# Local attention in a two-layer decoder: one exponential per tile, and products of two head groups in alternation

## The chip, the cores and the metric

The kernel runs on one core of a Trainium2 chip. The metric is the device time of one execution in microseconds (us). The engines are called PE (matrix products), PEld (PE's weight loads), DVE (vector), ACT (scalar), POOL (GpSimd) and SP (which issues DMAs). Each engine works through its own queue in order; a semaphore holds an instruction until what it needs is done.

## What is computed

1024 tokens of width 256 pass through two decoder layers. Only the fourth of the six parts, the local attention of the second layer, changes in its code. It splits each sequence of 256 tokens into 16 blocks of 16, and every block attends to itself, causally, with 8 heads of 64:

```python
qkv = lax.conv_general_dilated(xp, conv_w, window_strides=(1,), padding='VALID', ...) + conv_b
q, k, v = jnp.split(qkv, 3, axis=-1)
...
qh = jnp.einsum('bsd,dhk->bshk', qb, wq) + bq
kh = jnp.einsum('bsd,dhk->bshk', kb, wk) + bk
vh = jnp.einsum('bsd,dhk->bshk', vb, wv) + bv
...
scores = jnp.einsum('bqhk,bshk->bhqs', qh * scale, kh)
scores = jnp.where(causal[None, None], scores, jnp.asarray(-1000000000.0, scores.dtype))
attn = jax.nn.softmax(scores, axis=-1)
ctx = jnp.einsum('bhqs,bshk->bqhk', attn, vh)
mha_out = jnp.einsum('bqhk,hko->bqo', ctx, wo) + bo
...
out = mha_out @ proj_w + proj_b
```

The parts ahead of it are a linear attention, four experts, and a layer that fetches 64 rows of a table per token ("gather" below). The parts behind it are a cross attention with quantised queries, keys and weights over all 1024 tokens (16 heads), and 16 routed experts of which each token takes two.

## The kernel before

The tokens are 8 tiles of 128. The parts are written as Python generators (streams). A small planner, `Clock` (line 52), keeps an estimated time for each engine; `weave` (line 117) always continues the stream that could start first by that estimate, and what it emits goes into the engines' queues in just that order. PE, ACT and DVE keep this order; SP's and GpSimd's issues are placed by the scheduler behind it. `note` (line 81) holds the estimated costs, with `COLUMN` the price of a column of a matrix product, 0.00085 us at first and 0.0015 after `turn`.

The streams that matter here:

- `fetches` (line 689) issues the gather on GpSimd: 64 chunks of eight indirect DMAs, each chunk into one of three buffers `g`. `weigh` (line 700) uses a chunk: DVE multiplies it with `hb` and sums (`z`), ACT takes a tanh (`th`), DVE makes weights `blk`, PE forms eight products into the accumulator `accs`, in strips of 32 rows. Then the buffer is free for the chunk three further on. After 8 chunks a tile of tokens is complete (`added`).
- `locals_` (line 1037) then runs `local_attention` (line 902) on that tile, tile after tile. `queries` (line 997) follows with the queries of the cross attention, and three streams `units` (line 1051) work off its 8 x 16 pairs of tile and head: scores `psc` on PE in a pair of PSUM banks, maximum `mx` on DVE, exponential `e` on ACT, two transposes on PE in a single bank, a cast `qqT` on ACT, eight products into `accs`.
- `cross_out` and `routes` finish the tile; the routed experts (from line 1256) come after all streams.

`Banks` (line 163) hands out the PSUM banks. After `turn` (line 828) there are two pairs and three single banks (`banks(2, 2, 1, 1, 1)`, `bank.single = 4`); local attention and the units' transposes take single ones. A stream that finds none waits.

In `local_attention` the 128 tokens of a tile hold 8 blocks, so scores are taken over all 128 keys and a mask `cmask` (0 or -1e9) leaves the 16 of the own block. Heads lie as four pairs: head 2m+o has rows o*64 to o*64+63 of slice m in `qh` and `kh`. The projection is formed for the queries (part 0), then for the keys (part 1), each in its own bank and each read out by DVE before the next; a value product `pv` follows. Then two inner streams `half(0)` and `half(1)` are forked, one for each o: four score products, mask, maximum, four exponentials of 128 columns with a per-head bias and summed by the accumulator, reciprocal, product with it, four transposes, a copy `prT`, and four products `pc` into rows o*64 on of a bank, copied to `cT`. The output products `pm` and `po` end the tile.

The four exponentials of a half, line 957:

```python
for m in range(4):
    se_.activation(pr[:, m, :], pr[:, m, :], AF.Exp, bias=nm[:, m:m + 1], accum_out=sm[:, m:m + 1])
```

In the profile every instruction that passes through the planner has line 77, so groups are told apart by their tiles. A float32 product appears as two records.

Of the kernel before, what the change touches and what calls it, by code (L numbers as in the profile page):

```python
# [11 lines left out]
F32 = mybir.dt.float32  # L12
# [4 lines left out]
AF = mybir.ActivationFunctionType  # L17
ALU = mybir.AluOpType
AX = mybir.AxisListType
PSUM = bass.MemoryType.PSUM  # L20

P = 128
# [12 lines left out]
AH, AW, ABLK = 8, 64, 16  # L35
# [9 lines left out]
def bc(ap, axis, n):  # L45

    shape = list(ap.shape)
    shape.insert(axis, n)
    return ap.unsqueeze(axis).to_broadcast(shape)


class Clock:
# [14 lines left out]
    class _Engine:  # L67
# [3 lines left out]
        def __getattr__(self, op):  # L71
            emit = getattr(self.engine, op)

            def timed(*args, **kw):
                out = args[0] if args else kw["out"]
                self.clock.note(self.name, op, out, args, kw)
                return emit(*args, **kw)  # L77

            return timed

    def note(self, engine, op, out, args, kw):
        if engine == "sync":
            return
        n, late = math.prod(out.shape[1:]), 0.11
        if engine == "tensor":
            wide = (args[2] if op == "matmul" else args[1]).dtype == F32
            cost, late = max(0.11, n * self.COLUMN) if wide else max(0.03, n * self.COLUMN / 2), 0.17
            if out.shape[0] == 32:
                cost = max(0.06, n * self.COLUMN / 4)
        elif engine == "scalar":  # L90
            scaled, summed = hasattr(kw.get("scale"), "tensor"), "accum_out" in kw
            cost = 0.06 + n * 0.00083 + 0.23 * (scaled or summed) + 0.06 * (scaled and summed)
        elif engine == "gpsimd":
            cost = 1.23
        elif op in ("max", "max_index", "tensor_reduce"):
            src = args[1] if op != "max_index" else args[2]
            cost = (0.15 if op == "max_index" else 0.085) + 0.00104 * math.prod(src.shape[1:])
        elif op == "reciprocal":
            cost = 0.05 + 0.0064 * n
        elif op == "tensor_tensor_scan":  # L100
            cost = 0.1 + 0.0022 * n
        else:
            cost = 0.085 + (0.00054 if op in ("tensor_scalar", "tensor_copy") else 0.00104) * n
        begin = max(self.free[engine], self.t)
        for x in (*args[1:], *kw.values()):
            if hasattr(x, "tensor"):
                at, by = self.made.get(x.tensor.name, (0.0, engine))
                begin = max(begin, at + self.HOP * (by != engine))
        self.free[engine] = begin + cost
        done = begin + cost + late  # L110
        for x in (out, kw.get("accum_out")):
            if x is not None:
                self.made[x.tensor.name] = done, engine
        self.end = max(self.end, done)
        self.last = engine
# [89 lines left out]
def decoder(ctx, tc, a, out):  # L205


    nc = tc.nc
    ck = Clock(nc)
# [14 lines left out]
    def load(pool, name, shape, view=None, dtype=F32):  # L224
        s = pool.tile(shape, dtype, name="w_" + name, tag="w_" + name)
        nc.sync.dma_start(s, a[name] if view is None else view)
        return s
# [600 lines left out]
    def turn():  # L828

        yield "vector", lambda: None if 0 in fronts_left or 2 in fronts_left or not kv_done else max(kv_done[0], known[5])  # L830
        bank.closing = True
        yield "vector", lambda: None if bank.held else 0.0
        banks(2, 2, 1, 1, 1)
        even_ctx.close()
        wb = ctx.enter_context(tc.tile_pool(name="wb", bufs=1))
        A.conv_w = load(wb, "conv_w", [P, 2, 3 * 192], rows("conv_w"))
        A.conv_bqk = load(wb, "conv_bqk", [P, 1])
        A.conv_bv = load(wb, "conv_bv", [AW, 1])
        A.wqk = load(wb, "wqk", [P, AH * AW])
        A.bq = load(wb, "bq", [P, 4])  # L840
        A.bk = load(wb, "bk", [P, 4])
        A.wv = load(wb, "wv", [AW + 1, AH * AW])
        A.wo = load(wb, "wo", [P, 4, AW], rows("wo"))
        A.bo = load(wb, "bo", [AW, 1])
        A.proj_w = load(wb, "proj_w", [AW + 1, D])
        A.wq = load(wb, "wq", [P, 2, D], rows("wq"))
        A.bq_b = load(wb, "bxq", [P, D], a["bxq"].to_broadcast([P, D]))
        A.work = ctx.enter_context(tc.tile_pool(name="work", bufs=1))
        A.q3 = A.work.tile([P, XH, 4, XD], BF16, name="q3", tag="q3")
        nc.vector.memset(A.q3, 0.0)  # L850

        A.vT = A.work.tile([AW + 1, P], F32, name="vT", tag="vT")
        nc.vector.memset(A.vT[AW:AW + 1, :], 1.0)
        A.mT = A.work.tile([AW + 1, P], F32, name="mT", tag="mT")
        nc.vector.memset(A.mT[AW:AW + 1, :], 1.0)

        A.xp = [A.work.tile([P, 2, P + 2], F32, name=f"xp{i}", tag=f"xp{i}") for i in range(2)]
        nc.vector.memset(A.xp[0][:, :, 0:2], 0.0)
        A.turned = ck.end
        bank.single = 4  # L860
        ck.COLUMN = 0.0015
        yield "vector", None
# [39 lines left out]
    def local_attention(t):  # L902
# [15 lines left out]
        se_.activation(vT[0:AW, :], pqk[0:AW, 1, :], AF.Identity, bias=A.conv_bv)  # L918
        bank.give(pqk)
        yield "tensor", None  # L920
        qh = work.tile([P, 4, P], F32, name="qh", tag="qh")
        kh = work.tile([P, 4, P], F32, name="kh", tag="kh")
        for part, lo in ((0, 0), (1, AW)):
            p = yield from bank.take([P, 4, P])
            for m in range(4):
                te_.matmul(p[:, m, :], A.wqk[lo:lo + AW, m * P:(m + 1) * P], qk[lo:lo + AW, :], start=True, stop=True)
            yield "vector", None
            if part == 0:

                for m in range(4):  # L930
                    ve_.tensor_scalar(qh[:, m, :], p[:, m, :], A.bq[:, m:m + 1], 0.125, ALU.add, ALU.mult)
            else:
                ve_.tensor_tensor(kh, p, bc(A.bk, 2, P), ALU.add)
            bank.give(p)
            yield "tensor", None
        pv = yield from bank.take([P, AH * AW])
        te_.matmul(pv, vT, A.wv, start=True, stop=True)
        yield "scalar", None
        vh = work.tile([P, AH * AW], F32, name="vh", tag="vh")
        se_.copy(vh, pv)  # L940
        bank.give(pv)
        cT = work.tile([P, 4, P], F32, name="cT", tag="cT")

        def half(o):

            psc = yield from bank.take([P, 4, P])
            for m in range(4):
                te_.matmul(psc[:, m, :], qh[o * AW:(o + 1) * AW, m, :], kh[o * AW:(o + 1) * AW, m, :], start=True, stop=True)
            yield "vector", None
            pr = work.tile([P, 4, P], F32, name="pr", tag="pr", bufs=2)  # L950
            ve_.tensor_tensor(pr, psc, bc(cmask.rearrange("p g j -> p (g j)"), 1, 4), ALU.add)
            bank.give(psc)
            nm = work.tile([P, 4], F32, name="nm", tag="nm", bufs=2)
            ve_.tensor_reduce(nm, pr, AX.X, ALU.max, negate=True)
            yield "scalar", None
            sm = work.tile([P, 4], F32, name="sm", tag="sm", bufs=2)
            for m in range(4):
                se_.activation(pr[:, m, :], pr[:, m, :], AF.Exp, bias=nm[:, m:m + 1], accum_out=sm[:, m:m + 1])
            yield "vector", None
            ve_.reciprocal(sm, sm)  # L960
            ve_.tensor_tensor(pr, pr, bc(sm, 2, P), ALU.mult)
            yield "tensor", None
            tp = yield from bank.take([P, 4, P])
            for m in range(4):
                te_.transpose(tp[:, m, :], pr[:, m, :], ident)
            yield "scalar", None
            prT = work.tile([P, 4, P], F32, name="prT", tag="prT", bufs=2)
            se_.copy(prT, tp)
            bank.give(tp)
            yield "tensor", None  # L970
            pc = yield from bank.take([P, 4, P])
            for m in range(4):
                h = 2 * m + o
                te_.matmul(pc[o * AW:(o + 1) * AW, m, :], vh[:, h * AW:(h + 1) * AW], prT[:, m, :], start=True, stop=True)
            yield "scalar", None
            se_.copy(cT[o * AW:(o + 1) * AW], pc[o * AW:(o + 1) * AW])
            bank.give(pc)

        yield "tensor", None
        yield from ck.fork(half(0), half(1))  # L980
        yield "tensor", None
        pm = yield from bank.take([AW, P])
        for m in range(4):
# [456 lines left out]
```

## Time and profile before

| what | us |
|---|---|
| median of 3 runs | 1138.81 (1138.35 to 1142.45) |
| profiled execution | 1261.94 |
| its span | 1260.2 |
| first gather issue on GpSimd | 112.0 |
| start of local attention's first step for tile 0 (`xp` copied) | 421.7 |
| last gather issue | 971.0 |
| last products of the gather, `accs<-g,blk` | 997.5 |
| start of the last tile's output product (`w_proj_w`) | 1049.4 |
| first product of the routed experts' map (`pmap`) | 1143.1 |

The profiled execution took 123 us more than the median. The mean granted clock of PE was 0.708 of full speed.

The profile's page gives busy time and instruction count of each engine, and groups of instructions with their busy time, the mean duration of one in ns, and the engine's idle time ahead of them with what ended it. The busy time of a group is the union of its records: where records run side by side, it is less than their number times their mean. Further views list waits (who waited for whom: us in total, times, longest), busy times by stretch, and the instructions in order of time.

### The profile page before, as it was taken

To read this page: it belongs to the slowest core of one execution; us is meant where nothing else is said; L and a number is where in the kernel's file an instruction comes from. 1 tells how busy PE (TensorE), PEld (TensorE's weight loads), DVE (VectorE), ACT (ScalarE), POOL (GpSimd) and SP (SyncE) were. 2 spreads that over 40 slices of the span, in tenths; PEclk is the share of its full clock that TensorE was granted. 3 is DMA by queue.
4 is the path that set the end of the run, shared out by engine and by line. 5 is a ranking of instruction groups with operands and counts; after the bars stand their busy time and mean duration, and the time that the engine had idled before them with its cause. 6 is when DMAs were issued, how large, how long until landed. Compare 5 with 4: busy or idle time off the path is not lost. (4 is left out here: it accounts for less than half of the span.)

```text
span 1260.2 us, 15565 instructions
## 1 busy us (share of the span) xinstructions
PE 846.4 (67%) x4945; PEld 520.3 (41%) x4945; DVE 821.5 (65%) x2437; ACT 514.4 (41%) x1039; POOL 571.3 (45%) x589
## 2 busy tenths in 40 slices
PE   4672488627834686765688677676786699856990
PEld 3561365414622464333345334343353365323550
DVE  5568667596578458896677775767776767633222
ACT  1241033302301143453575643757456586731220
POOL 2003656575566556576465664655665000002314
PEclk8885588857965877565667866667777566556995
DMA  5012456666556446668665564555665230001323
GB/s 200 1 39 58 135 140 168 188 169 165 138 162 173 134 134 168 172 175 251 167 173 160 162 182 134 149 147 145 179 168 159 87 136 1 5 4 47 84 65 107
DMA packets 68640, 164.67 MB, mean 131 GB/s; under 512 B 15131, under 2 KB 32780, under 8 KB 68557
## 3 DMA queue, kind: packets, MB, share of 16 engines
q0 software_dynamic: 34688, 105.94, 29.9%
q1 hardware_dynamic: 33868, 57.72, 16.6%
q8 instruction: 40, 0.66, 0.2%
q14 instruction: 44, 0.35, 0.1%
HBM read 156.93 MB, written 6.68 MB: 130 GB/s over the span
## 5 line engine op out<-in xcount | busy, mean ns | idle before, releaser
L77 POOL DMA_INDIRECT g<-in_table,idxT x512 | 524.7, 1025 | 438.2 <-issue 153.4
L77 DVE TENSOR_REDUCE mx<-bank 128x1 f32<-128x1024 f32 x128 | 155.8, 1217 | 65.9 <-PE bank L77 51.7
L77 ACT ACTIVATE e<-bank,nb,qs_q 128x1024 uint8<-128x1024 f32 x128 | 154.3, 1206 | 56.1 <-DVE nb L77 22.0
L77 PE MATMUL accs<-g,blk 128*32 128x256 f32 x1024 | 103.9, 542 | 96.5 <-DVE blk L77 69.8
L77 ACT CAST qqT<-bank 128x1024 bf16<-128x1024 uint8 x128 | 127.6, 1010 | 87.9 <-PE bank L77 52.1
L77 PE MATMUL bank<-kT,qT 64*128 64x512 bf16 x256 | 104.2, 518 | 20.8 <-ACT e L77 15.4
L1312 POOL DMA_INDIRECT xr<-xs,smap x24 | 22.7, 948 | 189.5 <-DVE smap L1299 148.4
L77 PEld LDWEIGHTS accs<-g,blk 128*32 128x32 f32 x1024 | 34.5, 141 | 147.3 <-DVE blk L77 77.1
L77 PE MATMUL bank<-ident,e 128*128 128x128 f32 x256 | 72.6, 387 | 32.1 <-ACT e L77 19.0
L77 PE MATMUL accs<-vi,qqT 128*128 128x16 bf16 x1024 | 47.5, 174 | 56.6 <-ACT qqT L77 34.9
L77 DVE TENSOR_TENSOR g<-g,hb 128x1024 f32<-128x1024 f32 x64 | 78.3, 1223 | 8.7 <-issue 5.5
L77 PEld LDWEIGHTS <-qqT 128*128 128x128 bf16 x1024 | 39.8, 103 | 103.7 <-ACT qqT L77 58.9
L77 DVE TENSOR_REDUCE z<-g 128x8 f32<-128x1024 f32 x64 | 78.1, 1220 | 2.2
L77 PEld LDWEIGHTS bank<-ident,e 128*128 128x128 f32 x256 | 36.0, 185 | 85.6 <-issue 35.1
L77 ACT ACTIVATE th<-u 128x16 f32<-128x16 f32 x64 | 13.9, 218 | 90.8 <-DVE u L77 82.0
L77 PE MATMUL bank<-ident,ln_xn 128*128 128x128 f32 x96 | 25.0, 378 | 33.3 <-ACT ln_xn L77 17.1
L77 ACT ACTIVATE ln_xn<-x,ln_nmr,ln_rstd 128x256 f32<-128x256 f32 x48 | 27.0, 595 | 37.4 <-DVE ln_nmr L77 33.1
L77 PE MATMUL bank<-xnT,w_w_up 128*128 128x256 f32 x128 | 35.8, 441 | 7.6 <-ACT xnT L77 4.3
L1321 PE MATMUL ph<-w,xrT 128*128 x96 | 38.9, 513 | 1.8 <-DVE xrT L1318 1.7
L77 PE MATMUL bank<-w_ctxT,aT 128*128 128x256 f32 x128 | 34.3, 421 | 6.7 <-issue 5.1
L77 DVE TENSOR_SCALAR nb<-mx,nsq,ln 128x1 f32<-128x1 f32 x128 | 34.9, 273 | 4.6
L1325 DVE TENSOR_TENSOR hd<-hd,ph 128x176 f32<-128x176 f32 x24 | 8.0, 337 | 42.9 <-ACT hd L1324 42.9
(293 smaller groups left out, 1686.3 us busy)
## 6 DMA issues: line engine op xcount, KB each, us to landing
hb<-hdram SPq DMA_DIRECT2D x128, 256.0 KB
g<-in_table,idxT POOLq DMA_INDIRECT x512
w<-in_w SPq DMA_DIRECT2D x16, 352.0 KB
ys<-yr SPq DMA_DIRECT2D x24, 128.0 KB
w_w2a<-in_w SPq DMA_DIRECT2D x1, 2048.0 KB
x<-in_x SPq DMA_DIRECT2D x8, 128.0 KB
w_ctxT<-in_ctxT SPq DMA_DIRECT2D x1, 1024.0 KB
w_w_up<-in_w_up SPq DMA_DIRECT2D x1, 1024.0 KB
```

The costliest lines, as they stand in the source:

```text
L77: return emit(*args, **kw)
L1312: nc.gpsimd.indirect_dma_start(out=xr, out_offset=None, in_=xs, in_offset=bass.IndirectOffsetOnAxis(ap=smap[:, i:i + 1], axis=0))
L1321: nc.tensor.matmul(ph.rearrange("p j n -> p (j n)"), xrT[:, k, :], w13[:, bass.ds(e, 1), k, :], start=(k == 0), stop=(k == 1))
L1325: nc.vector.tensor_tensor(hd, hd, ph[:, 1, :], ALU.mult)
```

## The change

The local attention of a tile is rewritten as one stream without the fork.

- The products of o = 0 (rows 0 to 63) and o = 1 (rows 64 to 127) are issued in alternation, in two banks, for the projections (queries and keys) and for the scores; the products of the values alternate between output rows 0 to 63 and 64 to 127 of one bank.
- The query bias is added in one DVE operation of 512 columns, with a bias scaled beforehand (`bq8`).
- After the mask, DVE takes the maximum over the 8 key blocks of a row, which leaves the 16 columns of the own block for each of 8 heads (`sc`, 128 columns), then the maximum over these, and subtracts it. ACT takes one exponential of the 128 columns. DVE sums, inverts, multiplies, and spreads the result back to 8 x 128 columns by a product with a 0/1 mask `seen`.
- The value product `pv` stands behind the scores. `cT` is copied at once.
- `note` counts a product that is marked `halves` at 0.55 of its cost; `COLUMN`, `HOP`, `LANDS` and the other constants stay.

```diff
+                kw.pop("halves", None)
                 return emit(*args, **kw)
...
+            elif kw.pop("halves", False):
+                cost *= 0.55
...
+        A.bq8 = wb.tile([P, 4], F32, name="bq8", tag="bq8")
+        nc.vector.tensor_scalar(A.bq8, A.bq, 0.125, None, ALU.mult)
...
+        A.seen = A.work.tile([P, P // ABLK, ABLK], F32, name="seen", tag="seen")
+        nc.vector.tensor_scalar(A.seen, cmask, -0.5, None, ALU.is_ge)
...
+        p = []
+        for part in range(2):
+            p.append((yield from bank.take([P, 4, P])))
+        for m in range(4):
+            for part in range(2):
+                lo = part * AW
+                te_.matmul(p[part][:, m, :], A.wqk[lo:lo + AW, m * P:(m + 1) * P], qk[lo:lo + AW, :],
+                           start=True, stop=True, halves=True)
+        yield "vector", None
+
         qh = work.tile([P, 4, P], F32, name="qh", tag="qh")
+        ve_.scalar_tensor_tensor(qh, p[0], 0.125, bc(A.bq8, 2, P), ALU.mult, ALU.add)
+        bank.give(p[0])
         kh = work.tile([P, 4, P], F32, name="kh", tag="kh")
...
+        ve_.tensor_tensor(kh, p[1], bc(A.bk, 2, P), ALU.add)
+        bank.give(p[1])
+        yield "tensor", None
+
+        psc = []
+        for o in range(2):
+            psc.append((yield from bank.take([P, 4, P])))
+        for m in range(4):
+            for o in range(2):
+                te_.matmul(psc[o][:, m, :], qh[o * AW:(o + 1) * AW, m, :], kh[o * AW:(o + 1) * AW, m, :],
+                           start=True, stop=True, halves=True)
+        yield "vector", None
+        pr = work.tile([P, AH, P // ABLK, ABLK], F32, name="pr", tag="pr")
+        for o in range(2):
+            ve_.tensor_tensor(pr[:, 4 * o:4 * o + 4].rearrange("p m g j -> p m (g j)"), psc[o],
+                              bc(cmask.rearrange("p g j -> p (g j)"), 1, 4), ALU.add)
+            bank.give(psc[o])
+
+        sc = work.tile([P, AH, ABLK], F32, name="sc", tag="sc")
+        ve_.tensor_reduce(sc, pr.rearrange("p h g j -> p h j g"), AX.X, ALU.max)
+        sm = work.tile([P, AH], F32, name="sm", tag="sm")
+        ve_.tensor_reduce(sm, sc, AX.X, ALU.max)
+        ve_.tensor_tensor(sc, sc, bc(sm, 2, ABLK), ALU.subtract)
+        yield "tensor", None
         pv = yield from bank.take([P, AH * AW])
         te_.matmul(pv, vT, A.wv, start=True, stop=True)
         yield "scalar", None
+        se_.activation(sc, sc, AF.Exp)
...
+        ve_.tensor_reduce(sm, sc, AX.X, ALU.add)
+        ve_.reciprocal(sm, sm)
+        ve_.tensor_tensor(sc, sc, bc(sm, 2, ABLK), ALU.mult)
+        ve_.tensor_tensor(pr, bc(sc, 2, P // ABLK), bc(A.seen, 1, AH), ALU.mult)
...
+        pc = yield from bank.take([P, 4, P])
+        for m in range(4):
+            for o in range(2):
                 h = 2 * m + o
...
+                te_.matmul(pc[o * AW:(o + 1) * AW, m, :], vh[:, h * AW:(h + 1) * AW], prT[o][:, m, :],
+                           start=True, stop=True, halves=True)
+        yield "scalar", None
+        cT = work.tile([P, 4, P], F32, name="cT", tag="cT")
+        se_.copy(cT, pc)
```

More of the change, by code (lines that the diff above doesn't have):

```diff
@@ L922, in local_attention @@
+        bank.give(p[0])
         kh = work.tile([P, 4, P], F32, name="kh", tag="kh")
[L923 to L935, printed above, removed]
+        ve_.tensor_tensor(kh, p[1], bc(A.bk, 2, P), ALU.add)
@@ L941, in local_attention @@
         bank.give(pv)
[L942 to L962, printed above, removed]
+        yield "vector", None
@@ L963, in half @@
+        ve_.tensor_reduce(sm, sc, AX.X, ALU.add)
+        ve_.reciprocal(sm, sm)
+        ve_.tensor_tensor(sc, sc, bc(sm, 2, ABLK), ALU.mult)
+        ve_.tensor_tensor(pr, bc(sc, 2, P // ABLK), bc(A.seen, 1, AH), ALU.mult)
+        yield "tensor", None
+        prf = pr.rearrange("p h g j -> p h (g j)")
+        prT = []
+        for o in range(2):
             tp = yield from bank.take([P, 4, P])
             for m in range(4):
-                te_.transpose(tp[:, m, :], pr[:, m, :], ident)
+                te_.transpose(tp[:, m, :], prf[:, 4 * o + m, :], ident)
@@ L966, in half @@
             yield "scalar", None
-            prT = work.tile([P, 4, P], F32, name="prT", tag="prT", bufs=2)
-            se_.copy(prT, tp)
+            prT.append(work.tile([P, 4, P], F32, name="prT", tag=("qh", "kh")[o]))
+            se_.copy(prT[o], tp)
             bank.give(tp)
             yield "tensor", None
-            pc = yield from bank.take([P, 4, P])
-            for m in range(4):
+        pc = yield from bank.take([P, 4, P])
+        for m in range(4):
+            for o in range(2):
@@ L973, in half @@
                 h = 2 * m + o
[L974 to L980, printed above, removed]
+                te_.matmul(pc[o * AW:(o + 1) * AW, m, :], vh[:, h * AW:(h + 1) * AW], prT[o][:, m, :],
+                           start=True, stop=True, halves=True)
@@ L981, in local_attention @@
+        yield "scalar", None
+        cT = work.tile([P, 4, P], F32, name="cT", tag="cT")
+        se_.copy(cT, pc)
+        bank.give(pc)
         yield "tensor", None
```

## The prediction

> **What bounds the kernel now.** I read the busy shares first, then what GpSimd waits for, then busy times by stretch, then the local attention's own instructions, then one stall in order of time, and last the chain of waits of the end.
>
> ```profile
> PE 846.4 (67%) x4945; PEld 520.3 (41%) x4945; DVE 821.5 (65%) x2437; ACT 514.4 (41%) x1039; POOL 571.3 (45%) x589
> ...
> L77 PE MATMUL accs<-g,blk 128*32 128x256 f32 x1024 | 103.9, 542 | 96.5 <-DVE blk L77 69.8
> ...
> L77 PE MATMUL bank<-xnT,w_w_up 128*128 128x256 f32 x128 | 35.8, 441 | 7.6 <-ACT xnT L77 4.3
> ```
>
> No engine is full over the span, so the limit must be looked for by stage. From 112 to 972 us GpSimd issues 512 indirect gathers in 64 chunks of eight. Each chunk takes three buffers in turn, so chunk n starts only when the products `accs<-g,blk` of chunk n-3 are done.
>
> ```profile
> POOL g L77 <- PE accs L77: 113.7, 28, 9.6
> ```
>
> In order of time on GpSimd, a chunk's eight gathers take 10.3 us in the mean, and the pause ahead of a chunk that isn't late is about 1.3 us: 11.6 us is GpSimd's own pace. I summed what the pauses have above 1.3 us: 79 us from 412 us on, and 68 of these lie inside the seven stretches in which a local attention (tiles 0 to 6) is under way. The busy times by stretch show the same: GpSimd has 31.50 of 58 us (54%) while tile 5's local attention runs, and 19.22 of 27 us (71%) between two of them.
>
> ```profile
> 826.00:884.00 58.00, 44.58 (x343) 26.80 (x344) 40.48 (x85) 36.42 (x72) 31.50 (x32) 0.75 0.53 146
> 924.00:967.00 43.00, 35.16 (x259) 22.96 (x258) 32.32 (x56) 28.69 (x59) 28.45 (x28) 0.80 0.57 162
> ...
> 562.00:589.00 27.00, 12.69 (x98) 5.35 (x98) 20.79 (x65) 13.05 (x25) 19.22 (x19) 0.54 0.79 233
> ```
>
> (Columns: stretch, its length, busy us of PE, weight loads, DVE, ACT, POOL, then granted clock, DMA share, GB/s.) One stall, of tile 3:
>
> ```profile
> 690.42 2.72 PE L77 MATMUL bank<-kh,qh 64*128 64x128 f32 x15
> ...
> 693.07 1.50 PE L77 MATMUL accs<-g,blk 128*32 128x256 f32 x16
> ...
> 694.96 0.95 POOL L77 DMA_INDIRECT g<-in_table,idxT  x1 [8.49 <-PE bank L77]
> ```
>
> The chunk's weights `blk` were ready at 690.0, but its products stood in PE's queue behind 3.0 us of score products (690.04 to 693.07), and GpSimd got its buffer only after them. Earlier the same chunk had lost time in ACT's queue (its tanh waited from 683.3 to 688.6 behind a cast that waited for PE).
>
> The second place is the tail. Tile 7's last chunk is added at 998.25; its local attention runs to about 1050, its queries to 1069, then 16 units of its cross attention to 1117, then routing and the expert stage (1138 to 1260), which the change doesn't touch. Everything up to about 421 us is the same order as before.
>
> **The change part by part, per tile.**
>
> ```profile
> L77 ACT ACTIVATE pr<-pr,nm 128x128 f32<-128x128 f32 x64 | 24.8, 393 | 3.1 <-DVE nm L77 3.1
> L77 PE MATMUL bank<-kh,qh 64*128 64x128 f32 x128 | 24.7, 429 | 0.0
> ...
> L77 PE MATMUL bank<-qk,w_wqk 64*128 64x128 f32 x128 | 22.3, 321 | 11.0 <-ACT qk L77 9.3 <-DVE qh L77 1.1 <-issue 0.5
> L77 PE MATMUL bank<-prT,vh 128*64 128x128 f32 x128 | 20.5, 326 | 0.2 <-ACT xnT L77 0.2
> ```
>
> ACT: eight exponentials go, 24.8 / 8 = 3.1 us a tile (each one's accumulator read overlaps the next). One of 128 columns without accumulator comes: between the row of 64 columns (0.26) and the 0.39 of 128 columns with accumulator, I take 0.32. Two copies into `cT` of 0.58 become one of 128x512, 0.58 by the row of `vh`. ACT loses 2.8 + 0.6 = 3.4 us.
>
> PE: 67.5 us in the three rows above, 8.4 a tile, is to run two products at a time. The trace has such a pair: while tile 3's halves meet (691.07 to 691.9) records of the two halves start between each other, and each half keeps its own step of 0.213 us. Four strips of 32 columns are the other row: 103.9 / 1024 = 0.101 us a record against 35.8 / 128 = 0.280 for full 256-column records, 2.8 times for four strips, 69% of ideal. For two I take 1.7 times: 8.4 becomes 4.9, 3.5 us less. Bounds: 0 (no overlap) to 4.2 (twice).
>
> Here a rule speaks against the gain. "TensorE: Matmul & The Clock Gate" (Part 1, on the clock gate) says that the array's clock is halved unless recent activity holds it up. The rows agree in direction: PE busy 47% goes with a clock of 0.54 (562:589), 82% with 0.80 (924:967), a slope of 0.26 / 0.35. Taking 3.5 us out of about 57 us of stretch is 6 points of busy time, by that slope 0.045 of clock, so the other 33 us of PE in the stretch would take 2 us longer: 1.5 us gained instead of 3.5. But a low clock also lengthens what is counted as busy, and the gaps in these stretches come from waits that the change shortens; I keep 3.5 and let the range carry 1.5.
>
> DVE: out go four `qh` (9.0 / 8 = 1.1), two maxima of 0.69, two reciprocals (0.34), two products of 0.69; in come one `qh` of 512 (0.69 by `aT`), a maximum over 1024 (1.22 by `z<-g`), four operations of at most 128 columns (0.28 or so each), a reciprocal (0.20) and a product of 1024 (1.22). 6.3 becomes 6.5 us: no gain on the engine that is busiest by count, 425 of 598 us between 400 and 998. The maximum reads one float in 16. "SBUF — State Buffer" (the note on cachelines in the port section) says that reads which leave a 16-byte line each time pay; no row here has such a read by DVE. By the row it is 1.22; if the read costs double, 2.44, which is 10 us of DVE over eight tiles. I take 1.22, the row of the same count, and keep both.
>
> What moves: the value product stands behind the scores now; PE's scores wait for both `qh` and `kh`; the exponential waits for the maxima of all eight heads. Behind the scores on PE stand the next chunk's `accs` and the units, so a late `kh` holds both; before, a late `qh` held them at the second projection in the same way. The two added setup operations of DVE (a scaled bias, a 0/1 mask) run once: 0.3 us. They stand at about 405 us, while the bias's load is issued at 238.5, so there is no wait. SP and GpSimd issue the same transfers; only some of SP's `hb`, `hdram` and `xs` change places.
>
> **The sum**, against the profiled execution (1261.9 us, span 1260.2):
>
> - Gather stage. A local attention has about 17.7 us of PE work, 8.1 of ACT and 10.4 of DVE with its normalisation, 36 in all; the change takes out 3.5 + 3.4 - 0.2 = 6.7, or 19%. In the stall shown, 3.0 us of scores would become 1.7, 1.3 of 7.2 us lost, again 18%. So I take 20% of the 68 us: 14 us. Bounds: 0, and all 6.7 us on seven tiles, 47.
> - Tail. Tile 7's exponentials are on the chain of the end for 2.6 us, of which 2.3 go; PE's three groups give 3.8 (2.2 + 2.6 + 3.9 become about 5), one copy 0.6. Against it the chain loses the overlap of its halves: mask and maxima take 3.2 us instead of 1.3 before the exponential can start, normalising 2.0 instead of 0.9. Net 6.7 - 3.0, about 4 us.
>
> 18 us of 1262, 1.4%. The runs without a profile have a median of 1138.8, 0.902 of the profiled one, and no view tells where the difference lies; with the same factor the gain is 16 us and the time **1122 us**. Its own range, from half to twice the gain: 1106 to 1131.
>
> **Rivals.**
>
> *Slower: banks.* Units and local attention share three single PSUM banks. Before, a projection held one; now two are held from the first projection to the mask (672.7 to 695.3 for tile 3), and the units' transposes, which keep a bank some 2 us through the cast, have one left. Against it: the scores of the two halves already held two, and the planner places takes when it thinks them free. PE's queue stands with a transpose that waits. With five units in that stretch and eight tiles, each us that they wait is 40 us: from 0.45 us on the 18 us are eaten, and at 1 us the sum is 22 us over: 1159 us.
>
> *No change: DVE.* If without a profile GpSimd is quicker than here, DVE at over 70% paces the stage and neither ACT nor PE matters; only the tail's 4 us stay: 1135, and with the doubled maximum 1144.
>
> *More: all stalls of the removed work go.* 47 + 7 = 54 us, 1090. For it: the waits sit exactly in those stretches. Against it: much of them is PE at half clock in the convolution and `w_wp` products, which stay.
>
> *The pairs don't overlap.* Then PE gives nothing, ACT alone half of it: 8 us, 1132.
>
> **How the numbers follow.** A measurement tells 0.5% (5.7 us) from no change. Forecast 0.51, more 0.09, no overlap 0.08: faster 0.68. DVE's case 0.12 for the same, 0.04 for slower with the doubled maximum; banks or an unlucky new order of the queues 0.16. The range 1096 to 1154 leaves out most of the "more" case and the bad half of the banks' case.
>
> **What would show it.** Right: records of `bank<-kh,qh` and `bank<-qk,w_wqk` starting in pairs, and the three groups busy for some 40 us (67.5 / 1.7); ACT's busy time down by about 27 us; GpSimd's pauses above 1.3 us after 412 us near 65 us instead of 79; `sc<-pr` at 1.22 us. Wrong: the wait of `g` for `accs` not smaller, transposes `bank<-ident,e` idle after a bank's release, the mean clock well below 0.708, or the last `accs<-g,blk` not earlier than 998.

## The result and the profile after

| what | before | changed |
|---|---|---|
| median, first chip | 1138.58 (1136.96 to 1142.45, 4 runs) | 1155.07 (1154.42 to 1159.61, 4 runs) |
| profiled execution | 1261.94 | 1159.61 |
| its span | 1260.2 | 1157.9 |
| first gather of chunk 22 | 395.3 | 358.8 |
| last products of the gather end | 998.1 | 894.9 |
| from there to the end of the span | 262.1 | 263.0 |

The changed kernel takes 1.015 of the time before, 95% interval 1.0119 to 1.0182: 16.5 us more, where 16 less were forecast. (A ratio here and below is taken over the undisturbed runs of both kernels, so it can differ a little from the ratio of the medians beside it.) The profiled executions can't be set against each other. The one of before took 123 us more than the median of its kernel and is none of its timed runs; on which chip it was taken is not on record. The one of the changed kernel took 4.5 us more than its median. By chunk 22 they are already 36.5 us apart, and up to there both kernels issue the same work in the same order.

The profile's page of the changed kernel, engines first, then the gather's products:

```profile
PE 812.9 (70%) x4945; PEld 494.7 (43%) x4945; DVE 826.2 (71%) x2423; ACT 490.7 (42%) x911; POOL 567.6 (49%) x589
...
L78 PE MATMUL accs<-g,blk 128*32 128x256 f32 x1024 | 100.5, 529 | 80.1 <-DVE blk L78 75.1
```

PE is busy 33.5 us less and ACT 23.7 less; DVE has 4.7 more. The mean granted clock is 0.713, before 0.708. These differences too are between executions of different length; pairs from one chip follow in the part on the prediction. The groups that the prediction sized, from the groups of the changed kernel:

```profile
L78 DVE TENSOR_REDUCE sc<-pr 128x128 f32<-128x1024 f32 x8 | 15.0, 1872 | 0.3
...
L78 PE MATMUL bank<-prT,vh 128*64 128x128 f32 x128 | 14.7, 400 | 0.0
...
L78 PE MATMUL bank<-kh,qh 64*128 64x128 f32 x128 | 13.0, 340 | 1.3 <-DVE kh L78 1.3
...
L78 PE MATMUL bank<-qk,w_wqk 64*128 64x128 f32 x128 | 11.7, 287 | 0.9 <-ACT qqT L78 0.6
...
L78 DVE TENSOR_TENSOR pr<-sc,seen 128x1024 f32<-128x1024 f32 x8 | 9.8, 1225 | 0.3
...
L78 ACT ACTIVATE sc<-sc 128x128 f32<-128x128 f32 x8 | 2.5, 316 | 11.2 <-DVE sc L78 11.2
```

The three product groups are busy for 39.4 us instead of 67.5, and the exponential takes 0.316 us. The maximum that reads one float in 16 takes 1.872 us, while the spread of the same 1024 columns takes 1.225. The last row also shows a new wait: ACT idles 1.4 us a tile until DVE has the maximum of all eight heads.

GpSimd's wait for the buffers, and the busy times of the gather stage from chunk 23 on and of the rest:

```profile
POOL g L78 <- PE accs L78: 65.5, 28, 7.1
```

```profile
382.00:895.00 513.00, 391.82 (x2842) 222.70 (x2834) 419.06 (x1053) 284.29 (x487) 335.53 (x332) 0.69 0.67 180
895.00:1157.00 262.00, 185.29 (x877) 101.03 (x877) 120.09 (x356) 106.82 (x210) 38.21 (x41) 0.66 0.21 64
```

(Same columns as in the prediction.) In this stage DVE is busy 419 of 513 us (82%), PE 76%, GpSimd 65%. The wait of `g` is 65.5 us against 113.7. Most of that belongs to the condition of the execution, which the next part is about: on the two chips where both kernels have a profile, this wait falls by 15.6 us (130.8 to 115.2, chip B) and 15.9 us (144.3 to 128.4, chip D).

### The profile page after: what moved, and what is told of

Read it like the earlier page. It is cut to its first block, busy times and chain, and to the rows that moved or that the text cites. A ratio compares the mean times of both kernels' runs of the same rounds, so it can differ in the third digit from the quotient of the medians.

```text
span 1157.9 us, 15402 instructions
## 1 busy us (share of the span) xinstructions
PE 812.9 (70%) x4945; PEld 494.7 (43%) x4945; DVE 826.2 (71%) x2423; ACT 490.7 (42%) x911; POOL 567.6 (49%) x589
## 5 line engine op out<-in xcount | busy, mean ns | idle before, releaser
L78 PE MATMUL accs<-g,blk 128*32 128x256 f32 x1024 | 100.5, 529 | 80.1 <-DVE blk L78 75.1
L78 PE MATMUL bank<-kT,qT 64*128 64x512 bf16 x256 | 106.7, 522 | 33.5 <-ACT e L78 29.0
L78 PE MATMUL bank<-ident,e 128*128 128x128 f32 x256 | 73.9, 388 | 23.2 <-ACT e L78 15.2
L78 DVE TENSOR_TENSOR g<-g,hb 128x1024 f32<-128x1024 f32 x64 | 78.3, 1224 | 10.3 <-DMA g<-in_table,idxT 5.7
L78 PE MATMUL accs<-vi,qqT 128*128 128x16 bf16 x1024 | 47.2, 175 | 27.1 <-ACT qqT L78 24.6
L78 PEld LDWEIGHTS <-qT 64*128 64x128 bf16 x256 | 17.3, 101 | 54.6 <-issue 46.9
L1347 DVE TENSOR_TENSOR hd<-hd,ph 128x176 f32<-128x176 f32 x24 | 8.0, 336 | 42.8 <-ACT hd L1346 42.8
L78 PEld LDWEIGHTS bank<-ident,ln_xn 128*128 128x128 f32 x96 | 13.6, 182 | 55.1 <-ACT ln_xn L78 38.6
```

The lines of the kernel that those rows point to most:

```text
L1347: nc.vector.tensor_tensor(hd, hd, ph[:, 1, :], ALU.mult)
```

## Two conditions of the same kernel

On every other chip that was used, the kernel before took 1268 to 1295 us (medians; on the last chip two runs at 1271 and 1277), close to its first profiled execution and not to its 1138. It is not the profiler that makes it slow there: the medians of A to D are over 23 to 55 runs, and a profiled one among them does not stand out (on B 1284.54 beside 1292.93). Their profiles have waits that the views put down to "remote": no instruction of the program ends them. The list of waits of the kernel before, on the second of these chips (us in total, times, longest):

```profile
ACT qqT L77 <- remote: 39.5, 9, 8.4
...
ACT kT L77 <- remote: 21.8, 2, 13.5
...
ACT qk L77 <- remote: 14.0, 1, 14.0
```

All such waits in the list come to 175 us there, and to 139 in the profile that the prediction was read from (sums over the engines, over 200 rows; the rest adds up to 4 us). In the profile of the changed kernel on the first chip there is none. In the other 19 profiles each is a wait of ACT, DVE or GpSimd, none begins before the first gather is issued, and none ends more than 2.2 us after the last one. In the profile that the prediction was read from, 57 us of them lie ahead of chunk 22. One of them in order of time, in the changed kernel as it is, on the second chip:

```profile
132.68 0.79 PE L78 MATMUL bank<-headones,rk 128*128 128x8 f32 x3
...
142.49 0.95 POOL L78 DMA_INDIRECT g<-in_table,idxT  x1 [0.30 <-issue]
146.30 0.19 DVE L78 TENSOR_SCALAR rden<-bank 128x32 f32<-128x32 f32 x1 [10.99 <-remote]
146.39 1.01 ACT L78 COPY kT<-bank 128x1024 bf16<-128x1024 bf16 x1 [11.09 <-remote]
```

and the same `rden` in the profile on the first chip:

```profile
135.44 0.18 DVE L78 TENSOR_SCALAR rden<-bank 128x32 f32<-128x32 f32 x1
```

`rden` needs the products `bank<-headones,rk`, which are done by 133.7 in both. On the first chip DVE goes on at 135.44; on the second it stands for 10.99 us, ACT beside it for 11.09, and both go on 2.9 us after the last of eight gathers has been issued (142.49 + 0.95). That the news of PE's work comes late while GpSimd issues is what this looks like ("late signals" in the recorded expectations); the trace doesn't show the cause.

Three marks, from GpSimd's instructions in order of time, one execution each ("pauses" is what GpSimd's pauses ahead of chunks 23 to 64 have above 1.3 us, "remote" all waits of that kind):

| execution | chunk 22 | pauses | last products | from there to the end | remote |
|---|---|---|---|---|---|
| before, first profile | 395.3 | 79.5 | 998.1 | 262.1 | 139 |
| changed, first chip | 358.8 | 33.6 | 894.9 | 263.0 | 0 |
| before, chip B | 401.5 | 102.1 | 1022.4 | 260.3 | 175 |
| changed, chip B | 404.9 | 83.2 | 1014.1 | 263.3 | 173 |
| before, chip D | 401.7 | 106.4 | 1024.6 | 259.6 | 179 |
| changed, chip D | 403.1 | 90.8 | 1017.6 | 260.3 | 155 |

Over six profiles of the kernel before the pauses run from 79.5 to 106.4 us; a seventh, of an execution of 1300.78 us, has 113.8. That is wider than the 14 us which the prediction wanted to see move.

## The experiments

Five more chips, A to E; "before" is the kernel before on the same chip. Theories: *pairs and banks* (the alternating products hold two single banks, the units wait), *DVE* (it paces the stage, and the change adds to it), *order* (the planner's estimate places the queues badly), and *chip* (the forecast was read from waits that the first chip doesn't have). The recorded expectations also name *chain* (the one stream has a longer chain of dependent steps than two halves side by side) and *landing* (the gathers' data land late). The kernel before against itself tells how far a ratio can be trusted: 0.9949 (0.9909 to 0.9989) on A, 1.0016 (0.9984 to 1.0048) on B and 1.0045 (1.0004 to 1.0087) on C. Ratios of different chips that lie less than a per cent apart are not told apart.

### Chip A: one part undone

The kernel before itself.

> The kernel before, unchanged, for a second profile: in the first one the gathers of the second chunk landed 10 us later than in the changed kernel's profile, before the two orders part. If that was that one execution (A), this profile has a span near 1137 us and the last products of the gather at about 875 us, and its pauses of GpSimd above 1.3 us are far below 79 us after the turn. If the profile itself slows this kernel (B), the span is again near 1260.

1293.35 us beside 1288.81. Its profile is the one with 113.8 us of pauses and has 204 us of remote waits.

The changed kernel with full cost in the planner:

```diff
-                cost *= 0.55
+                cost *= 1.0
```

> The changed kernel with the same instructions; only the planner counts the paired products at their full cost again (factor 1.0 for 0.55). If the new order is what costs (order), the time moves by 5 us or more, either way. If the single softmax chain costs (chain) or the two held banks do (banks), it stays within 5 us of 1155.

1274.56 us, 0.9925 (0.9898 to 0.9952).

The changed kernel without alternation in its three places, both banks still held:

```diff
-        for m in range(4):
-            for part in range(2):
+        for part in range(2):
+            for m in range(4):
...
-                           start=True, stop=True, halves=True)
+                           start=True, stop=True)
```

> The changed kernel with the products of o = 0 ahead of those of o = 1, at full cost: no pairs, two banks held as before. If pairs help as forecast (3.5 us of PE a tile), this is 5 to 15 us slower than the changed kernel, 1160 to 1170. Chain: about the same as the changed kernel, 1155. Order: anything within 15 us of it, with no relation to the PE time that is lost.

1277.16 us, 0.995 (0.9921 to 0.998).

The kernel before with alternating projections and scores, the eight exponentials and the two inner streams kept:

```diff
+        p = []
+        for part in range(2):
+            p.append((yield from bank.take([P, 4, P])))
+        for m in range(4):
+            for part in range(2):
+                lo = part * AW
+                te_.matmul(p[part][:, m, :], A.wqk[lo:lo + AW, m * P:(m + 1) * P], qk[lo:lo + AW, :],
+                           start=True, stop=True, halves=True)
...
+        pscs = []
+        for o in range(2):
+            pscs.append((yield from bank.take([P, 4, P])))
```

> The kernel before with pairs in projection and scores, two banks held for both, and the forked halves with their eight exponentials left as they were. Chain: 1130 to 1138, as the loss lies in the new softmax. Banks: 1150 or more, as the two banks are held here too. Order: anywhere from 1125 to 1160.

1305.12 us, 1.0134 (1.0052 to 1.0216). The pairs alone bring no gain. The two versions with one exponential lie where the kernel before lies against itself here (0.9949): no loss is to be seen, against the measured 1.015 of the first chip. The changed kernel itself did not run on this chip, so what its pairs are worth can't be read here.

### Chip B: the changed kernel again, and the estimate

> The kernel before, unchanged, to have its profile from the same chip as the three that follow. If gathers land fast here, a chunk's products on DVE start 10 to 12 us after its last issue, the time is near 1138 and the last products of the gather end near 875 us. If they land slowly, 18 to 22 us, near 1289 and 1030.

1293.29 us beside 1292.93.

The changed kernel as it is:

> The changed kernel, unchanged, beside the kernel before. Theory 'landing': the change's sign depends on how the gathers land; where they land slowly its stalls are those of the first profile, and it is 0.5 to 1.5% faster than before (ratio 0.985 to 0.995); where they land fast, 1.012 to 1.018. Theory 'chain': slower by 1% or more on both.

1285.65 us, 0.9986 (0.994 to 1.0031): the loss of the first chip is not there. That is neither the gain that *landing* wanted (0.985 to 0.995) nor the loss of 1% or more that *chain* wanted on every chip.

The kernel before, and after it the changed kernel, with a higher price of a column:

```diff
-        ck.COLUMN = 0.0015
+        ck.COLUMN = 0.0017
```

> The kernel before, but the planner counts a column of a product at 0.0017 us in place of 0.0015 after the turn: same instructions, other order. Theory 'order': moves by 0.5% or more, either way, as much as the change itself. Theories 'chain' and 'banks' : within 0.5% of before.

1289.89 us, 1.0007 (0.9968 to 1.0045).

> The changed kernel with a column at 0.0017 us. Theory 'order': moves by 0.5% or more against the changed kernel, either way, and may end below the kernel before. Theory 'chain' and 'banks': stays within 0.5% of the changed kernel.

1279.91 us, 0.9932 (0.9882 to 0.9982). The estimate moves the kernel before by nothing, where *order* expected 0.5% or more, and the changed one by half a per cent, with intervals that meet. On this chip there is no loss to be undone, so whether the order costs 1.5% on the first chip stays open.

### Chip C: the same three versions once more

> The kernel before on a third chip. Where PE's signals come without the long delays of the first profile (no stretch over 1.5 us with PE, DVE and ACT all idle between 110 and 1040 us, as in the changed kernel's profile), its time is near 1138 and its profile shows where it is ahead of the changed kernel: 'chain' expects that GpSimd pauses less while a local attention runs; 'order' that the gain lies in a few single stalls of weigh. Where the delays are there, near 1290.

1271.28 us beside 1267.72.

> The changed kernel without pairs (o = 0 ahead of o = 1, full cost). Where before is near 1138: 'chain' 1150 to 1160, like the changed kernel; 'pairs cost' 1138 or less; 'order' anything from 1130 to 1170. Where before is near 1290: ratio about 0.995, as on the first chip.

1275.2 us, 1.0179 (1.0076 to 1.0282).

> The kernel before with pairs in projection and scores only, eight exponentials kept. Where before is near 1138: 'chain' 1130 to 1140; 'banks' 1150 or more; 'order' anything from 1130 to 1170. Where before is near 1290: ratio about 1.013, as on the first chip.

1281.59 us, 1.0211 (1.0105 to 1.0317).

> The changed kernel with the planner's factor for pairs at 1.0: the same instructions in another order. Where before is near 1138: 'order' moves by 5 us or more from 1155; 'chain' and 'banks' stay within 5 us. Where before is near 1290: ratio about 0.99, as on the first chip.

1270.11 us, 1.0116 (1.0002 to 1.0231). The kernels with one exponential take what they took on A, within 0.4% (1275.2 and 1277.16; 1270.11 and 1274.56). The kernel before is 1.6% quicker here (1267.72 and 1288.81), and with it the sign of the ratio turns. The pairs alone are slower on both chips. The kernel before itself is not steady here: in a later session one run took 1286.95 us.

The kernel before once more on this chip:

> The kernel before, for its profile on a chip where signals between engines aren't late. There the time is near 1138, no wait is ended from outside the program's instructions ('remote' 0 us, as in the changed kernel's first profile, where the first profile of before has 139), and the last products of the gather end near 875 us: then the two profiles can be laid side by side. Otherwise near 1270 to 1290 with 130 us or more of such waits.

1273.13 us, with 91.0 us of pauses and 141 us of remote waits; the other profile of it on this chip has 101.0 and 187.

### Chip D: the two halves of the change

The changed kernel with the projections of queries and keys in one bank each, one read out and given back before the other is taken, as before:

```diff
-        for m in range(4):
-            for part in range(2):
-                lo = part * AW
-                te_.matmul(p[part][:, m, :], A.wqk[lo:lo + AW, m * P:(m + 1) * P], qk[lo:lo + AW, :],
-                           start=True, stop=True, halves=True)
+        for part, lo in ((0, 0), (1, AW)):
+            p = yield from bank.take([P, 4, P])
+            for m in range(4):
+                te_.matmul(p[:, m, :], A.wqk[lo:lo + AW, m * P:(m + 1) * P], qk[lo:lo + AW, :], start=True, stop=True)
...
+            bank.give(p)
```

> The changed kernel with the projection as before: the queries into one bank, read out and given back, then the keys into one bank. The scores and the values keep their alternating products, the softmax keeps its one exponential. Theory 'banks' (two single banks held from the projection on make the units' transposes wait): this is faster than the changed kernel on the same chip by 1% or more, 0.98 to 0.99 of it. Theory 'orders' (the planner places each version by an estimate that is off, and any edit draws a new order): it differs from the changed kernel by up to 1% either way, with no relation to the banks. Theory 'DVE' (DVE paces the gather stage and its work is the same here): within 0.5% of the changed kernel.

1319.45 us, 1.0215 (1.0135 to 1.0294).

The same, with scores in one bank at a time too and no alternation anywhere: one exponential alone.

> The changed kernel's softmax (one exponential of 128 columns, the spread by the mask) without any alternating products: projections, scores and values of o = 0 and then of o = 1, one single bank at a time in projection and scores. It is the other half of the version with the pairs alone, which was slower than before by 1.3% and 2.1%. Theory 'pairs' (the alternating products, with the two banks that they hold, cost what was lost): this is not slower than before, 0.985 to 1.00, and faster than the changed kernel on the same chip by 0.5% or more. Theory 'DVE' (the one exponential brings 0.65 us of DVE work a tile more than was counted, on the engine that is fullest): within 0.5% of the changed kernel or slower than it. Theory 'orders': anywhere within 1% of the changed kernel.

1306.24 us, 1.0085 (1.0048 to 1.0123).

> The changed kernel itself, so that the two versions beside it are compared with it on the same chip. It was 1.015 of before where that took 1138 us and 0.9986 where it took 1293. If the ratio goes with the condition of the chip: above 1.01 where before takes less than 1150 us, near 1.00 where it takes more than 1280.

1288.33 us, 0.9913 (0.9878 to 0.9948).

> The kernel before with a profile. Where it takes about 1138 us, the theory of late signals says: hardly any wait that nothing in the program ends (139 us in the first profile of before, 0 in that of the changed kernel), GpSimd's pauses above 1.3 us near 50 us over all chunks and not 123, the last products of the gather near 875 us. Where it takes 1260 us or more: 130 to 190 us of such waits, as in the other profiles.

1285.94 us, 179 us of remote waits. The waits of the version with one bank and then of one exponential alone; the changed kernel had 128.4 us in this row on the same chip:

```profile
POOL g L78 <- PE accs L78: 155.9, 29, 12.9
```

```profile
POOL g L78 <- PE accs L78: 161.3, 29, 13.3
```

The theory of banks wanted the first to be faster than the changed kernel. It is 3% slower. The second, which takes out all pairs, is 1.7% slower. Both are more than the 1% that *order* allowed. On this chip, where the complete change is even a little faster than before, each edit that takes a part out makes it worse, so neither part is found to cost anything here. Yet these two have also the most remote waits, 225 and 273 us against 155, so their ratios may say as much of this condition as of their work. Whether one bank costs time on the first chip was not measured.

### Chip E: a last profile of the kernel before

> The kernel before once more with a profile. Where it takes about 1138 us, the theory of late signals says: hardly any wait that nothing in the program ends, GpSimd's pauses above 1.3 us near 50 us over all chunks, the last products of the gather near 875 us. Where it takes 1260 us or more: 130 to 190 us of such waits, as in the other profiles.

1276.55 us, 172 us of remote waits. No second execution at 1138 us came, so the profile of before that would show the first chip's loss is missing.

## Why the prediction was wrong

**The stalls to be gained (14 us): the step that failed.** The prediction summed 68 us of pauses in one execution that took 1262 us, took 20% of them, and scaled the gain by 0.902, "the same factor", to a chip of which no view was at hand. The pauses of that execution are mixed with waits that no work of the program ends. In tile 0's local attention `qk` stood for one:

```profile
435.96 0.37 ACT L77 ACTIVATE qk<-bank,w_conv_bqk 128x128 f32<-128x128 f32 x1 [13.89 <-remote]
```

GpSimd's pauses ahead of the chunks at 441.2 and 458.1, 6.2 and 5.8 us above 1.3, are among the 68. In the changed kernel's profile on the first chip there are no such waits, and its pauses above 1.3 us are 33.6 us in all from chunk 23 on. A factor keeps each cause in proportion; here one cause is absent. In the condition that was read, the term itself was about right in size: pauses 18.9 us fewer on B and 15.6 on D. That is one pair of executions each, and the scatter of one kernel is larger. Even there the last products end only 8.3 and 7.0 us earlier. On D the eight gathers of chunks 22 to 64 themselves take 446.9 us instead of 436.7, and chunk 22 starts 1.4 us later; on B these are 3.0 and 3.4 us, and the last products follow the last gather 4.6 us later. A gain that isn't there makes the change even; that it takes 16.5 us more is a loss of its own, and its cause stays open (below).

**The tail (4 us): the chain became shorter as forecast, and the end did not come sooner.** In the three profiles of the changed kernel the stretch from the last products of the gather to the end is 263.0, 263.3 and 260.3 us; in seven of before 256.8 to 262.1, in the mean 259.4. No remote wait lies in this stretch in any profile, so it can be compared between executions. Times from the end of the last products, first before (first profile), then changed (first chip):

| step of the last tile | before | changed |
|---|---|---|
| `xp` copied | 6.7 | 12.9 |
| `qk` read out | 14.1 | 21.6 |
| first score product | 23.9 | 25.6 |
| first exponential | 28.9 | 30.7 |
| first transpose of `pr` | 32.8 | 36.7 |
| first value product | 38.3 | 47.7 |
| last copy `cT` done | 46.9 | 50.3 |
| last cast `qqT` of the units | 117.1 | 118.0 |

The first value product can't be compared as it stands: before, it belongs to the first half alone, and the second half follows. From `qk` to the last `cT` the local attention takes 32.8 us before and 28.7 in the changed kernel, 4.1 less, as the sum had it. The other profiles give 32.8 five times and 29.7 once for before, and 28.7 in both others of the changed kernel. But 7.5 us are lost ahead of `qk`. The instructions in order of time, before:

```profile
998.25 0.42 DVE L77 TENSOR_TENSOR x<-accs,x 128x256 f32<-128x256 f32 x1 [0.70 <-PE accs L77]
...
1003.45 0.60 ACT L77 ACTIVATE ln_xn<-x,ln_nmr,ln_rstd 128x256 f32<-128x256 f32 x1 [0.62 <-DVE ln_nmr L77]
...
1004.84 0.37 ACT L77 COPY xp<-bank 128x256 f32<-128x256 f32 x1
...
1012.18 0.37 ACT L77 ACTIVATE qk<-bank,w_conv_bqk 128x128 f32<-128x128 f32 x1 [2.01 <-PE bank L77]
...
1044.39 0.58 ACT L77 COPY cT<-bank 64x512 f32<-64x512 f32 x1 [0.83 <-PE bank L77]
```

and changed:

```profile
895.12 1.22 DVE L78 TENSOR_REDUCE mx<-bank 128x1 f32<-128x1024 f32 x1
...
896.56 0.41 DVE L78 TENSOR_TENSOR x<-accs,x 128x256 f32<-128x256 f32 x1
...
903.84 0.59 ACT L78 ACTIVATE ln_xn<-x,ln_nmr,ln_rstd 128x256 f32<-128x256 f32 x1
...
907.78 0.40 ACT L78 COPY xp<-bank 128x256 f32<-128x256 f32 x1
...
916.50 0.37 ACT L78 ACTIVATE qk<-bank,w_conv_bqk 128x128 f32<-128x128 f32 x1 [4.58 <-PE bank L78]
...
944.59 0.58 ACT L78 COPY cT<-bank 128x512 f32<-128x512 f32 x1 [1.05 <-PE bank L78]
```

The sum `x<-accs,x` now stands in DVE's queue behind a maximum of a unit, and its normalisation among more maxima and another tile's; ACT copies `xp` only after further exponentials and casts. That it is the planner's order which does this was tested: the version with full cost in the planner has the same instructions, and there (chip A, last products done at 1014.9) `xp` is copied at 6.7 us again:

```profile
1021.64 0.37 ACT L78 COPY xp<-bank 128x256 f32<-128x256 f32 x1
...
1028.14 0.37 ACT L78 ACTIVATE qk<-bank,w_conv_bqk 128x128 f32<-128x128 f32 x1 [1.16 <-PE bank L78]
...
1053.73 0.61 ACT L78 COPY cT<-bank 128x512 f32<-128x512 f32 x1
```

There `cT` is done 39.4 us after the last products (41.0 on C), in the kernel before 43.0 to 46.9, and still the stretch to the end is 257.3 us (259.6 on C), inside the range of the kernel before. The pairs alone have `cT` at 38.6 us and the end at 259.7. So the step that failed in the tail is the path: a shorter chain up to `cT` was counted in full as an earlier end, and in these versions no earlier end comes out of the scatter. What sets the end instead stays open; 16 units of the last tile follow this chain.

**PE's pairs (1.7 times): right.** 67.5 us became 39.4, 1.71 times; between profiles of one chip it is 65.9 to 43.0 (B) and 67.1 to 42.8 (D), 1.53 and 1.57 times. The rival in which they don't overlap is out: without alternation, in the version with one exponential alone, the groups are busy for 27.4 + 21.7 + 18.9 = 68.0 us on D.

**ACT: right.** 23.7 us fewer (23.6 on B, 24.6 on D), forecast about 27. The exponential took 0.316 us for 0.32, the copy of `cT` 0.584 for 0.58.

**DVE ("no gain"): a size off.** `sc<-pr` was taken from the row of the same count at 1.22 us; it takes 1.872, 0.65 more, 5.2 us over the tiles. The upper bound of 2.44 held it. The Trainium skill's "SBUF — State Buffer" (the note on cachelines in the port section) warned that such a read pays; here it is 1.53 times. In all, DVE has 8.5 us more on B and 7.9 on D, where some 2 were forecast. This lands on a full engine: on B DVE's busy time in the gather stage rises from 429.4 to 440.2 us, while PE's falls from 436.4 to 422.3. The seven maxima of this stage make 4.6 us of that more than was counted; work that the new order puts ahead of the last products is another part.

**PE's gain of 3.5 us a tile, and the clock: too large.** The prediction named a rule that would leave 1.5 us of the 3.5 and kept 3.5. The engines' totals of before and changed on chip B:

```profile
PE 846.9 (66%) x4945; PEld 516.9 (40%) x4945; DVE 821.0 (64%) x2437; ACT 514.7 (40%) x1039; POOL 569.9 (44%) x589
```

```profile
PE 836.6 (65%) x4945; PEld 504.1 (39%) x4945; DVE 829.5 (65%) x2423; ACT 491.1 (38%) x911; POOL 572.6 (45%) x589
```

The three groups lose 22.9 us there, PE as a whole 10.3; on D it is 24.3 and 8.1. That is 1.0 to 1.3 us a tile, one pair of executions each, while the seven profiles of before scatter from 834.3 to 853.7. The clock was lower: in the mean of the runs that the ratios are taken over, 0.697 against 0.703 on B and 0.696 against 0.703 on D. Whether less work of PE is the reason is not shown. The version with one exponential alone, which keeps PE's work, also has 0.697 on D, and the pairs with full cost have 0.704 beside 0.704 on A. The 0.713 of the changed kernel on the first chip has no profile of before in the same condition beside it.

**The rivals.** "Slower: banks" has the sign and nearly the time (1159). But what was to show it is small: ahead of the transposes `bank<-ident,e` PE is idle for 23.2 us, before 32.1. Of that, 3.9 us are waits for the read-out of `qh`. The transposes don't use `qh`, so it is its bank, one of the two now held, that they wait for:

```profile
PE bank L78 <- DVE qh L78: 3.9, 3, 2.7
```

and 2.3 us wait for a cast that frees a bank, before 9.5. That is five stalls on banks, not one for each of 40 units, and holding one bank in the projections was slower on D. That 1159 lies close to the result is luck, as far as the runs show. "No change: DVE", with the doubled maximum, gave 1144: its premise, a quicker GpSimd with DVE above 70%, is what the first chip shows (82%), but it falls 11 us short, and no run separates it there.

**What stays open.** Which part costs 16.5 us on the first chip. If the tail of before is as long there as in its other profiles (259 us in the mean), its last products end at about 1138.6 - 1.7 - 259 = 878 us, 17 earlier than the changed kernel's 894.9: then the loss lies in the gather stage. That is an estimate. DVE's share and the queues' new order are both candidates, waits on held banks a smaller one; none was shown. No version was found that beats both kernels: with the column price of 0.0017 the changed kernel takes 0.9932 on B, where the change itself is even, but it has not run on the first chip.

## What to carry to other kernels

Before a stall is priced, see whether the profiled execution takes the time of the median; at 11% above it, look first for waits that nothing in the program ends, and don't scale a gain from one condition to the other. In a kernel whose queues are ordered by a planner, work that is taken from one engine is worth what the new order leaves of it: list the steps of the last tile with their times before and after, up to the end. Here a chain that became 4.1 us shorter began 7.5 us later, and in a version where it ended earlier, the end of the kernel did not. An edit of a few microseconds on a tile needs its comparison on more than one chip.

## What was not expected of the hardware

- The same kernel takes 1138 us on one chip and 1268 to 1295 on five others; all its profiles at 1260 us or more have 139 to 204 us of waits that the trace puts down to nothing in the program, and the one profile near 1138, of the changed kernel, has none.
- A change can have another sign on another chip: 1.015 (1.0119 to 1.0182) on the first, 0.9913 (0.9878 to 0.9948) on D.
- These waits all lie between the first gather's issue and 2.2 us after the last one's; the stretch behind the gather takes 256.8 to 262.1 us in seven profiles of the kernel before.
- A DVE maximum over 1024 floats in steps of 16 takes 1.872 us, in sequence 1.220 (`z<-g`).
